# Queries and keys produced with features on partitions, RoPE by a lane shuffle

## The chip, the cores and the metric

The kernel runs on one core of one Trainium2 chip. The metric is the device time of one execution in microseconds (us). The core has a matrix engine (TensorE, PE in the profile, with its weight loads as PEld), a vector engine (VectorE, DVE), an activation engine (ScalarE, ACT), a general engine (GpSimd, POOL), and a queue engine (SyncE, SP) that here issues all DMAs. Each engine works through its own instructions in order; semaphores make one wait for another. Tiles lie in SBUF on 128 partitions; products land in PSUM banks of 128 x 512 f32.

## The reference

Everything is f32. x is 4 sequences of 512 tokens with 1024 features. Layernorms have no weights.

```python
x = x + layernorm(attention(layernorm(x)))
x = x + layernorm(ffn(layernorm(x)))

# attention: 32 query heads, 8 key/value heads of 32 features
qkv = x @ w_qkv.T + b_qkv                 # 1024 + 256 + 256 columns
q, k = apply_rope(q), apply_rope(k)       # turns pairs of features by a position's angle
scores = q @ k.T / sqrt(32), causal; out = softmax(scores) @ v
return out @ w_o.T + b_o

# ffn: a plain product plus 8 experts of rank 16, two chosen per token
result = x @ base_w.T + base_b
result += 2 * sum over e of w_full[e] * (x @ lora_A[e].T) @ lora_B[e].T
```

## The kernel before

**Tokens and staging.** The 2048 tokens are 16 tiles of 128, in the program `tokens`; four tiles are one sequence, and tile i of a sequence (i from 0 to 3) sees i + 1 blocks of keys. For each tile x is loaded (`xa`), normalised, and transposed on TensorE (`transposes`, line 562) to `T_xn`, which has features on partitions. The same is done for the input of the ffn (`T_h`). Tiles are worked on in pairs. The first tile of the last sequence is attended last.

**Products.** `project` (line 577) makes 128 x 512 of a product: for each of 8 (or 4) chunks of 128 features, one matmul with the tokens as the stationary operand (128 x 128, loaded as weights) and 512 weight columns moving (line 587). So the result has tokens on partitions. A pair of tiles goes through `seven` (line 626): the 2 x 2 block product of two tiles by two feature halves by two column halves is made with 7 block products in place of 8. It needs sums of input tiles (`s_q`, `s_o`, `s_f`, in `parts`) and mixed weight blocks, which `mix` makes at the start and writes to DRAM. Each of the 7 has 4 steps of one matmul. Bank results are added into the output tiles on VectorE (line 698); the bias and the difference of the bias's halves (`bias_step`) come in there. Bias tiles are copies of the row on all 128 partitions (`bqkv_sb`, 768 KB by one DMA). The first pair, and single tiles elsewhere, go through `whole`: 8 steps for each half of the columns. Weight pieces of 128 x 512 (`piece`) stream in through a ring of 14.

**Keys and values.** `keys_values` (line 888) makes k and v of a tile together: 8 steps with 512 columns (256 of k, 256 of v). VectorE adds the biases, v to its tile and k to `raw_k`; then come RoPE, two transposes on TensorE (line 929) and two copies to `kT`, which has features on partitions.

**Queries.** `queries` (line 953) makes q into `raw_q`, tokens on partitions, in two halves of 512 columns; then come RoPE, four transposes a half (line 980) and one copy on ScalarE to `qT` with the factor 1/sqrt(32) (line 987).

**RoPE.** The columns of a head are sorted, first components first. `rotate` (line 729) has VectorE multiply the swapped halves by sin (two instructions at line 740, into `turn`), then GpSimd multiply `raw` by cos in place (line 751), then VectorE add the two (line 756). `turn` has one buffer, `raw` six, shared by q and k.

**Attention.** A group is 4 heads, one from each quarter of the partitions, or 8 or 16 where a tile sees only two blocks of keys or one. `scores` (line 1347) makes the products of `qT` and `kT` in four PSUM banks that belong to all groups in turn (`sc`); VectorE adds the mask (line 1416) and takes maxima (line 1426), ScalarE takes exps with sums (line 1376), GpSimd scales (line 1390), TensorE transposes (line 1440), ScalarE or VectorE copies, and `values` multiplies by v (line 1463).

**What sets the order.** The order on every engine is fixed when the program is built. `Order` (line 90) plays the work through with an assumed duration for each instruction and appends each to its engine when its turn comes. On TensorE the scores come first, then the transposes (`turn_lanes`), then the values, then the dense products (`gl_lane`, `kv_lane`, `main_lane`), whichever is ready. `main_lane` is a fixed sequence: q of the first pairs, then for each pair its output product, q of the pair two later, and its ffn. On the other engines an instruction has an urgency (0 first). PSUM outside `sc` has 4 banks, taken and given by `banks`. SP issues the loads in the order of `all_loads` (line 1491) with the pieces between: x of the first tile, the k and v weights, then the qkv bias, then the RoPE table.

Of the kernel before, what the change touches and what calls it, by code (L numbers as in the profile page):

```python
# [260 lines left out]
def kernel(  # L261
# [34 lines left out]
    kvpool = ctx.enter_context(tc.tile_pool(name="kvpool", bufs=4))  # L296
# [12 lines left out]
    qT_slots, kT_slots, raw_slots, turn_slots = Slots(8), Slots(4), Slots(6), Slots(1)  # L309
# [55 lines left out]
    bqkv_sb = const.tile([P, QKV], F32, name="bqkv_sb")  # L365
# [13 lines left out]
    def loads(what):  # L379
# [16 lines left out]
    biases = {  # L396
        "q": bqkv_sb,
        "o": bo_sb,
        "f": bbase_sb,
    }  # L400
    bias_steps = {name: const.tile([P, 512], F32, name=f"bias_step_{name}") for name in plain}
# [39 lines left out]
    def bias_step(name):  # L441
        yield loaded["b", name]
        b = biases[name]
        yield combine(
            4, lambda: bias_steps[name], lambda: b[:, 512:D], lambda: b[:, :512], ALU.subtract
        )
        has_bias[name].finish(order.at)
# [150 lines left out]

    def with_pieces(used, steps):
        for piece, step in zip(used, steps):  # L600
            step.piece = piece
            start(piece.used(step.done))
        return steps

    def whole(name, tok_name, k, lhsT, ready, take, room, used=None, more=None):

        used = used or block(name, plain, 0, k) + block(name, plain, 1, k)
        needs = [[ready[c // 4], used[c].here] for c in range(ND)]
        needs[0] += room
        if more:  # L610
            needs.append(more[2])
        return with_pieces(
# [13 lines left out]
    def seven(name, pair_name, tiles, ready, out, room, ended, free, more=None):  # L626
# [17 lines left out]
        def parts(taken):  # L644
# [15 lines left out]
        bias = biases[name]  # L660
# [13 lines left out]
            (lambda: bias[:, :512], c11, None),  # L674
            (c11, c21, None),
            (c11, c11, None),
            (lambda: bias_steps[name], c22, None),
# [30 lines left out]
        for k, (lhs, wants, of, h, half) in enumerate(blocks):  # L708
# [11 lines left out]
            def w(c, used=used, extra=extra):  # L720
                return used[c].sb if c < H else extra[1]

            steps += with_pieces(
                used,
                project(lhsT, w, 512, f"{name}_{pair_name}_{k}", needs, partial(take, k)),
# [3 lines left out]
    def rotate(raw, n, i, name):  # L729

        nh, half = n // HD, HD // 2
        yield turn_slots.take()
        turn = ropes.tile([P, 512], F32, tag="turn", name=f"turn_{name}")
        raw3, turn3 = (a[:, :n].rearrange("p (h d) -> p h d", d=HD) for a in (raw, turn))
        for a, b in ((0, half), (half, 0)):
            sin = rope_sb[:, i, 1, a : a + half].unsqueeze(1).to_broadcast([P, nh, half])
            yield dve(
                0.1 + n * 0.00065,
                2,
                lambda: nc.vector.tensor_tensor(  # L740
                    out=turn3[:, :, a : a + half],
                    in0=raw3[:, :, b : b + half],
                    in1=sin,
                    op=ALU.mult,
                ),
            )
        cos = rope_sb[:, i, 0, :].unsqueeze(1).to_broadcast([P, nh, HD])
        yield pool(
            0.2 + n * 0.0021,
            1,  # L750
            lambda: nc.gpsimd.tensor_tensor(out=raw3, in0=raw3, in1=cos, op=ALU.mult),
        )
        yield dve(
            0.1 + n * 0.0012,
            2,
            lambda: nc.vector.tensor_add(raw[:, :n], raw[:, :n], turn[:, :n]),
        )
        turn_slots.give(order.at)

    def new_raw(name):  # L760
        return ropes.tile([P, 512], F32, tag="raw", bufs=6, name=f"raw_{name}")


    class Sequence:
        def __init__(self, b):
            self.kT = [None] * NKT
            self.kT_taken = [kT_slots.take() for _ in range(NKT)]
            self.has_k, self.v, self.has_v = {}, {}, {}
            self.b = b
            self.left = [NQ * GROUP] * NKT  # L770
            self.left_v = NQ * ND

        def k_tile(self, kt):
            if self.kT[kt] is None:
                self.kT[kt] = kvpool.tile([P, S], F32, tag="kT", name=f"kT_{self.b}_{kt}")
            return self.kT[kt]
# [111 lines left out]
    def keys_values(job):  # L888
# [3 lines left out]
        raw, has_raw, k_ready = [], Task(), Task()  # L892

        def take_raw():
            yield [job.ready[0]] + seq.kT_taken
            yield v_slots.take()
            yield raw_slots.take()
            has_raw.finish(order.at)

        start(take_raw())  # L900

        def take(acc, done):
            yield done
            job.read(order.at)

            def v_issue():
                seq.v[i] = kvpool.tile([P, KVD], F32, tag="v", bufs=6, name=f"v_{t}")
                nc.vector.tensor_add(
                    seq.v[i], acc[:, KVD : 2 * KVD], bqkv_sb[:, D + KVD : D + 2 * KVD]
                )  # L910

            yield dve(0.41, 0, v_issue)
            seq.has_v[i].finish(order.at)
            raw.append(new_raw(f"k_{t}"))
            yield dve(
                0.1 + KVD * 0.00115,
                0,
                lambda: nc.vector.tensor_add(
                    raw[0][:, :KVD], acc[:, :KVD], bqkv_sb[:, D : D + KVD]
                ),  # L920
            )
            banks.give(order.at)
            yield from rotate(raw[0], KVD, i, f"k_{t}")
            k_ready.finish(order.at)

        def turn_k():
            pt = ps.tile([P, 4, P], F32, tag="ps", name=f"pt_k_{t}")
            for kt in range(NKT):
                nc.tensor.transpose(pt[:, kt, :], raw[0][:, kt * P : (kt + 1) * P], ident)

            def end():
                yield step_k.done
                raw_slots.give(order.at)
                for kt in range(NKT):
                    yield copy(
                        P,
                        lambda: seq.k_tile(kt)[:, i * P : (i + 1) * P],
                        lambda: pt[:, kt, :],
                    )
                banks.give(order.at)  # L940
                seq.has_k[i].finish(order.at)

            start(end(), order.now)

        step_k = Step(0.23, turn_k, [k_ready], bank=True)
        needs = [[job.ready[c // 4], loaded["kv", c]] for c in range(ND)]
        needs[0] += [has_raw, loaded["b", "q"]]
        products = project(
            lambda c: job.xnT()[:, c, :], lambda c: wkv_sb[:, c, :], 2 * KVD, f"kv_{t}", needs, take
        )  # L950
        return [step_k], products

    def queries(pair, used=None):

        raw, q_ready, steps_q = {}, {}, {}

        def take_room():
            yield q_job[pair[0]].ready[0]
            for _ in range(NH * len(pair)):
                yield qT_slots.take()  # L960
                yield raw_slots.take()
            has_room.finish(order.at)

        has_room = Task()
        start(take_room())

        def out(k, h):
            if (k, h) not in raw:
                raw[k, h] = new_raw(f"q_{pair[k].t}_{h}")
            return raw[k, h]  # L970

        def ended(k, h):
            yield from rotate(raw[k, h], 512, pair[k].i, f"q_{pair[k].t}_{h}")
            q_ready[k, h].finish(order.at)

        def turn_q(k, h):
            tok = pair[k]
            pt = ps.tile([P, 4, P], F32, tag="ps", name=f"pt_q_{tok.t}_{h}")
            for c in range(4):
                nc.tensor.transpose(pt[:, c, :], raw[k, h][:, c * P : (c + 1) * P], ident)  # L980

            def end():
                yield steps_q[k, h].done
                raw_slots.give(order.at)
                tok.qT[h] = qpool.tile([P, 4, P], F32, tag="qT", name=f"qT_{tok.t}_{h}")
                yield act(
                    0.6, 0, lambda: nc.scalar.activation(tok.qT[h], pt, AF.Copy, scale=QSCALE)
                )
                banks.give(order.at)
                tok.has_q[h].finish(order.at)  # L990

            start(end(), order.now)

        for k, h in [(0, 0), (0, 1), (1, 0), (1, 1)][: NH * len(pair)]:
            q_ready[k, h] = Task()
            steps_q[k, h] = Step(0.44, partial(turn_q, k, h), [q_ready[k, h]], bank=True)
        names = [q_job[tok] for tok in pair]
        if len(pair) == 2:
            steps = seven(
# [9 lines left out]
            return [[steps_q[0, 0], steps_q[0, 1]], [steps_q[1, 1]], [steps_q[1, 0]]], steps  # L1009

        def take(h, acc, done):
# [3 lines left out]
            cols = slice(h * 512, (h + 1) * 512)  # L1015
            yield dve(0.69, 0, lambda: nc.vector.tensor_add(out(0, h), acc, bqkv_sb[:, cols]))
# [15 lines left out]
        return [[steps_q[0, 0], steps_q[0, 1]]], steps  # L1032
# [314 lines left out]
    def scores(g):  # L1347
# [4 lines left out]
        for c in range(g.n):  # L1352
            for r in range(QUADS):
# [4 lines left out]
                    rhs=seq.kT[g.kt][rows, :n],  # L1358
# [42 lines left out]
        def softmax():  # L1401
# [4 lines left out]
            seq.left[g.kt] -= g.n  # L1406
            if not seq.left[g.kt]:
# [83 lines left out]
    def all_loads():  # L1491
# [10 lines left out]
        bias_q = load(("b", "q"), 768, bqkv_sb, b_qkv.broadcast_to([P, QKV]))  # L1502
# [7 lines left out]
        def chain():  # L1510
# [3 lines left out]
            yield from loads([bias_q, rotary])  # L1514
# [64 lines left out]
    kv_lane, gl_lane, main_lane = [], [], []  # L1579
    for job in jobs:  # L1580
# [118 lines left out]
```

## Time and profile before

| | |
|---|---|
| median of three runs | 1208.66 us (1207.46 to 1209.03) |
| the profiled execution | 1208.46 us, its span 1206.7 us |
| granted TensorE clock | 0.987 of full |
| TensorE matmul records | 7248 |
| transposes of q (line 980) | 128 |
| transposes of k (line 929) | 32 |
| records of q's products | 456 |
| records of k and v's products | 256 |

The span runs from the first to the last instruction. A line of instructions reads: line of the program, engine, operation, output<-inputs, shape, count; then busy time in us and the mean of one in ns; then the idle time of the engine just before, and who ended it. In a list of instructions by tile or line the three numbers are shortest, median and longest in ns, then the first and last start. A wait reads: who waited <- for whom, us in total, times, longest. A line of the timeline is start, length, engine, line, operation, and how many like it follow one another. A line of a window is its bounds and length, then busy us (and instructions) of PE, PEld, DVE, ACT and POOL, the granted clock, DMA share and GB/s. One f32 matmul of the program is two records, a transpose is one. Matmuls are pipelined, so the time of one record is longer than the distance to the next.

### The profile page before, as it was taken

How to read it: one execution, taken by the hardware profiler on the slowest of the kernel's cores; microseconds unless marked ns; L12 is line 12 of the kernel's file. 1: busy time of each engine (PE TensorE's matmuls, PEld its weight loads, DVE VectorE, ACT ScalarE, POOL GpSimd, SP SyncE). 2: the span in 40 equal slices, each digit the busy share in tenths (PEclk: the TensorE clock that was granted, in tenths of full speed). 3: DMA queues.
4: the chain of work that ended last, by engine and by line, in shares of the span. 5: the costliest groups of instructions: out<-in, count | busy, mean ns of one | idle time of the engine just before them, and what ended most of it. 6: DMA issues, size and time to landing. Idle time of an engine off the chain costs nothing.

```text
span 1206.7 us, 21495 instructions
## 1 busy us (share of the span) xinstructions
PE 1154.6 (96%) x7248; PEld 630.9 (52%) x7248; DVE 908.3 (75%) x1932; ACT 452.9 (38%) x1399; POOL 614.8 (51%) x801
## 2 busy tenths in 40 slices
PE   6999899999899999999999999999999999979997
PEld 3545454645556555565555555555555555536453
DVE  4687887987768977898777777789777897676453
ACT  0344443443435344345433233344433443344000
POOL 1575866753555645454745445445545572554211
PEclk9999899999999999999999999999999999988999
DMA  9768768665174445754367355853347644733783
GB/s 347 257 223 297 253 216 279 222 217 182 54 225 142 149 149 175 235 162 157 128 207 237 124 177 172 271 171 129 105 124 254 208 137 153 269 115 99 254 309 122
DMA packets 118316, 232.52 MB, mean 193 GB/s; under 512 B 13504, under 2 KB 14528, under 8 KB 118208
## 3 DMA queue, kind: packets, MB, share of 16 engines
q1 hardware_dynamic: 118208, 231.16, 58.1%
q8 instruction: 58, 0.95, 0.3%
q14 instruction: 50, 0.41, 0.1%
HBM read 210.14 MB, written 20.97 MB: 192 GB/s over the span
## 4 chain that ended last, share of the span: by engine, by line
PE 77%; DVE 13%; ACT 3%; POOL 3%; issue 2%; DMA 2%; SPq 0%; POOLq 0%; ACTq 0%
PE acc_f L587 17%; PE acc_o L587 16%; PE acc_q L587 11%; PE pt_p L1440 10%; PE acc_kv L587 7%; PE sc L1355 6%; PE av L1463 5%; DVE nmax L1426 3%; ACT pr L1376 3%; DVE sc L1416 2%; PE acc_gl L587 2%; POOL pr L1390 2%; PE pt_xn L562 1%; PE pt_h L562 1%; DVE w L533 1%
## 5 line engine op out<-in xcount | busy, mean ns | idle before, releaser
L1390 POOL TENSOR_SCALAR pr<-pr,rtot 128x256 f32<-128x256 f32 (+3 forms) x512 | 310.7, 620 | 296.1 <-DVE rtot L1385 205.6
L1376 ACT ACTIVATE pr<-sc,nmax 128x256 f32<-128x256 f32 (+3 forms) x512 | 264.5, 532 | 209.4 <-DVE sc L1416 83.0
L1426 DVE TENSOR_REDUCE nmax<-sc 128x2 f32<-128x768 f32 (+3 forms) x176 | 198.2, 1126 | 48.1 <-ACT pr L1376 45.4
L1440 PE MATMUL pt_p<-ident,pr 128*128 128x128 f32 x1280 | 181.4, 279 | 16.6 <-POOL pr L1390 9.6
L1440 PEld LDWEIGHTS pt_p<-ident,pr 128*128 128x128 f32 x1280 | 146.7, 142 | 85.7 <-issue 52.2
L330 ACT COPY prT<-pt_p 128x512 f32<-128x512 f32 (+1 forms) x212 | 112.3, 545 | 190.4 <-PE pt_p L1440 189.3
L587 PE MATMUL acc_kv<-wkv_sb,T_xn 128*128 128x512 f32 x256 | 117.1, 596 | 0.2 <-DVE w L698 0.2
L331 DVE COPY prT<-pt_p 128x512 f32<-128x512 f32 (+1 forms) x140 | 89.9, 643 | 34.9 <-PE pt_p L1440 33.1
L587 PE MATMUL acc_q<-piece,T_xn 128*128 128x512 f32 x224 | 105.9, 599 | 3.3 <-DMA piece<-in_w_qkv_dram 3.0
L587 PE MATMUL acc_f<-piece,T_h 128*128 128x512 f32 x232 | 108.4, 597 | 0.2 <-ACT prT L330 0.2
L1376 ACT ACTIVATION_READ_ACCUMULATOR pr<-sc,nmax 128x1 f32 x512 | 106.7, 208 | 0.0
L587 PE MATMUL acc_f<-piece,s_f 128*128 128x512 f32 x224 | 106.5, 595 | 0.1
L587 PE MATMUL acc_o<-piece,aT 128*128 128x512 f32 x232 | 105.8, 600 | 0.0
L1416 DVE TENSOR_TENSOR sc<-sc,cmask 128x256 f32<-128x256 f32 (+2 forms) x176 | 96.5, 548 | 10.4 <-ACT pr L1376 4.8
L1355 PE MATMUL sc<-kT,qT 32*128 32x384 f32 (+3 forms) x1024 | 96.5, 476 | 7.8 <-ACT pr L1376 7.6
L587 PE MATMUL acc_q<-piece,s_q 128*128 128x512 f32 x224 | 103.5, 595 | 0.1
L587 PE MATMUL acc_o<-piece,s_o 128*128 128x512 f32 x224 | 102.2, 593 | 0.0
L522 POOL TENSOR_TENSOR rstd<-veps,neg_half 128x1 f32<-128x1 f32 x64 | 35.5, 558 | 115.3 <-DVE veps L518 115.3
L1385 DVE RECIPROCAL rtot<-total 128x1 f32<-128x1 f32 (+2 forms) x352 | 53.9, 158 | 51.2 <-ACT pr L1376 49.1
L1463 PEld LDWEIGHTS av<-prT,v 128*32 128x32 f32 x2560 | 65.3, 109 | 51.2 <-issue 39.5
L1463 PE MATMUL av<-prT,v 128*32 128x128 f32 x2560 | 90.5, 276 | 0.0
L338 POOL TENSOR_TENSOR y<-y,w 128x512 f32<-128x512 f32 x60 | 79.4, 1334 | 17.1 <-DVE w L533 17.0
(146 smaller groups left out, 1390.0 us busy)
## 6 DMA issues: line engine op xcount, KB each, us to landing
piece<-in_w_o_dram SPq DMA_DIRECT2D x116, 256.0 KB, 3.5
piece<-in_w_base_dram SPq DMA_DIRECT2D x116, 256.0 KB, 3.6
piece<-mixed_q SPq DMA_DIRECT2D x112, 256.0 KB, 3.6
piece<-mixed_o SPq DMA_DIRECT2D x112, 256.0 KB, 3.8
piece<-mixed_f SPq DMA_DIRECT2D x112, 256.0 KB, 3.2
piece<-in_w_qkv_dram SPq DMA_DIRECT2D x100, 256.0 KB, 3.6
xa<-in_x_dram SPq DMA_DIRECT2D x32, 256.0 KB, 3.7
y<-in_x_dram SPq DMA_DIRECT2D x16, 512.0 KB, 4.8
```

The lines of the kernel that those rows point to most:

```text
L330: act=(0.15 + n * 0.00085, lambda: nc.scalar.copy(out(), in_())),
L331: dve=(0.15 + n * 0.00105, lambda: nc.vector.tensor_copy(out(), in_())),
L338: engine.tensor_tensor(out=out(), in0=in0(), in1=in1(), op=op)
L587: nc.tensor.matmul(acc[0][:, :n], lhsT=lhsT(c), rhs=w(c), start=(c == 0), stop=last)
L1355: nc.tensor.matmul(sc[:, r, c * n : (c + 1) * n], lhsT=tok.qT[g.kt][rows, (g.at + c) % GROUP, :], rhs=seq.kT[g.kt][rows, :n], start=True, ...
L1376: lambda: nc.scalar.activation(pr[:, c * n : (c + 1) * n], sc4[:, r, c, :], AF.Exp, bias=nmax[:, r, c : c + 1], accum_out=total[:, r, c : ...
L1385: yield dve(0.17, 1, lambda: nc.vector.reciprocal(rtot[:, r, : g.n], total[:, r, : g.n]))
L1390: lambda: nc.gpsimd.tensor_scalar(pr[:, c * n : (c + 1) * n], pr[:, c * n : (c + 1) * n], rtot[:, r, c : c + 1], 1.0, ALU.mult, ALU.mult,),
L1416: lambda: nc.vector.tensor_tensor(out=diag, in0=diag, in1=cmask.unsqueeze(1).unsqueeze(1).to_broadcast([P, q, g.n, P]), op=ALU.add,),
L1426: lambda: nc.vector.tensor_reduce(nmax[:, some, : g.n], sc4[:, some], AX.X, ALU.max, negate=True),
L1440: nc.tensor.transpose(pt[:, j, :], g.pr[r][:, j * P : (j + 1) * P], ident)
L1463: nc.tensor.matmul(av[r * HD : (r + 1) * HD, c, :], lhsT=g.seq.v[j][:, head * HD : (head + 1) * HD], rhs=g.prT[r][:, c * (i + 1) + j, :], ...
```

## The change

Products of q and k have the weights as the stationary operand and x moving. A step of q that was one matmul with 512 moving columns is four, each with 128 weight columns as stationary operand and the 128 tokens moving, into four quarters of the bank. Results have features on partitions, so the transposes and their copies are gone. q is accumulated in `qT` itself. k has 4 steps (two halves of 128 features, each in two steps of 4 matmuls), v has 4 steps with tokens stationary as before, 256 columns moving; they share one bank.

The biases of q and k are one number per partition: `bqk_sb`, 128 x 10, loaded from the row by a DMA of single elements; v's bias is a copy on all partitions. For q, VectorE adds it spread along the tokens; for k, ScalarE adds it while it copies from PSUM.

RoPE's swap of halves is a shuffle of 32 lanes on VectorE. The tables of sin and cos are turned once at the start: GpSimd repeats the 32 columns of each four times, TensorE transposes it (8 transposes in all), ScalarE copies it with the factor 32^(-1/4), so that q and k together carry 1/sqrt(32). GpSimd's cos multiply and VectorE's sin multiply both follow the shuffle. `turn` has two buffers. `kT` is one tile for a sequence. SP issues the table ahead of the biases.

```diff
+    def project_turned(x, w, name, needs, take):
...
+        def issue(c):
...
+            for f in range(4):
+                nc.tensor.matmul(
+                    acc[0][:, f, :],
+                    lhsT=w(c)[:, f * P : (f + 1) * P],
+                    rhs=x(c),
...
         ends = (
-            (lambda: bias[:, :512], c11, None),
+            (bias(biases[name]), c11, None),
...
-    def rotate(raw, n, i, name):
-
-        nh, half = n // HD, HD // 2
+    SWAP = [(d + HD // 2) % HD for d in range(HD)]
+
+    def rotate(raw, out, i, name):
...
+        def multiply(t, by, engine):
+            engine.tensor_tensor(out=t, in0=t, in1=by, op=ALU.mult)
+
+        yield dve(0.1 + n * 0.135, 2, lambda: nc.vector.stream_shuffle(turn, raw, SWAP))
+
+        def by_cos():
+            yield pool(0.2 + n * 0.27, 1, partial(multiply, raw, cos, nc.gpsimd))
+
+        has_cos = start(by_cos(), order.at)
+        yield [loaded["sin"]]
+        yield dve(0.1 + n * 0.145, 2, partial(multiply, turn, sin, nc.vector))
+        yield has_cos
         yield dve(
-            0.1 + n * 0.0012,
+            0.1 + n * 0.155,
             2,
-            lambda: nc.vector.tensor_add(raw[:, :n], raw[:, :n], turn[:, :n]),
+            lambda: nc.vector.tensor_tensor(out=out(), in0=raw, in1=turn, op=ALU.add),
         )
         turn_slots.give(order.at)
...
+    def rope_tables():
...
+                    nc.gpsimd.tensor_copy(
+                        wide[0].rearrange("p i (r d) -> p i r d", d=HD)[:, :NQ],
+                        rope_sb[:, :, at, :].unsqueeze(2).to_broadcast([P, NQ, QUADS, HD]),
+                    )
...
+                for i in range(NQ):
+                    nc.tensor.transpose(pt[:, i, :], wide[0][:, i, :], ident)
...
+                        lambda: nc.scalar.activation(
+                            to, pt[:, :NQ], AF.Copy, scale=math.sqrt(QSCALE)
+                        ),
...
     def keys_values(job):
...
+            if n < 4:
+                kt = n // 2
+                for c in range(4 * (n % 2), 4 * (n % 2) + 4):
+                    nc.tensor.matmul(
+                        acc[0][:, kt * P : (kt + 1) * P],
+                        lhsT=wkv_sb[:, c, kt * P : (kt + 1) * P],
+                        rhs=job.xnT()[:, c, :],
...
+            else:
+                for c in range(2 * (n - 4), 2 * (n - 4) + 2):
+                    nc.tensor.matmul(
+                        acc[0][:, half : half + KVD],
+                        lhsT=job.xnT()[:, c, :],
+                        rhs=wkv_sb[:, c, half : half + KVD],
...
+            for kt in range(NKT):
+                yield act(
+                    0.3,
+                    1,
+                    lambda: nc.scalar.activation(
+                        raw[:, kt, :],
+                        acc[:, kt * P : (kt + 1) * P],
+                        AF.Identity,
+                        bias=bqk_sb[:, ND + kt : ND + kt + 1],
+                    ),
+                )
+            start(keys(raw), order.at)
...
-        def turn_k():
-            pt = ps.tile([P, 4, P], F32, tag="ps", name=f"pt_k_{t}")
-            for kt in range(NKT):
-                nc.tensor.transpose(pt[:, kt, :], raw[0][:, kt * P : (kt + 1) * P], ident)
...
     def queries(pair, used=None):
...
         def ended(k, h):
-            yield from rotate(raw[k, h], 512, pair[k].i, f"q_{pair[k].t}_{h}")
-            q_ready[k, h].finish(order.at)
-
-        def turn_q(k, h):
             tok = pair[k]
-            pt = ps.tile([P, 4, P], F32, tag="ps", name=f"pt_q_{tok.t}_{h}")
-            for c in range(4):
-                nc.tensor.transpose(pt[:, c, :], raw[k, h][:, c * P : (c + 1) * P], ident)
...
+            yield [loaded["cos"], loaded["sin"]]
+            yield from rotate(out(k, h), lambda: out(k, h), tok.i, f"q_{tok.t}_{h}")
+            tok.has_q[h].finish(order.at)
...
-        bias_q = load(("b", "q"), 768, bqkv_sb, b_qkv.broadcast_to([P, QKV]))
+        biases_qkv = [
+            load(
+                ("b", "q"),
+                128,
+                bqk_sb,
+                b_qkv[:, : D + NKT * P].rearrange("o (f p) -> p (o f)", p=P),
+            ),
+            load("bv", 128, bv_sb, b_qkv[:, D + KVD :].broadcast_to([P, KVD])),
+        ]
...
-            yield from loads([bias_q, rotary])
+            yield from loads([rotary] + biases_qkv)
```

## The prediction

> **What bounds it now.** I read the page first: the busy line, then the chain that ended last.
>
> ```profile
> PE 1154.6 (96%) x7248; PEld 630.9 (52%) x7248; DVE 908.3 (75%) x1932; ACT 452.9 (38%) x1399; POOL 614.8 (51%) x801
> ...
> PE 77%; DVE 13%; ACT 3%; POOL 3%; issue 2%; DMA 2%; SPq 0%; POOLq 0%; ACTq 0%
> ```
>
> TensorE (PE) is full and holds 77% of the chain, so its bill comes first. Busy times overlap (a matmul drains while the next starts), so I price a record by the pitch of a run, from the timeline of TensorE in two windows (start, length, instructions):
>
> ```profile
> 602.35 3.60 PE L587 MATMUL acc_kv<-wkv_sb,T_xn 128*128 128x512 f32 x8
> 605.78 3.60 PE L587 MATMUL acc_f<-piece,s_f 128*128 128x512 f32 x8
> ...
> 611.67 1.91 PE L1440 MATMUL pt_p<-ident,pr 128*128 128x128 f32 x16
> 613.42 3.60 PE L587 MATMUL acc_f<-piece,T_h 128*128 128x512 f32 x8
> ```
>
> ```profile
> 240.63 2.12 PE L587 MATMUL acc_gl<-wgl_sb,T_h 128*128 128x136 f32 x16
> 242.59 0.59 PE L587 MATMUL acc_f<-piece,T_h 128*128 128x512 f32 x1
> ```
>
> A record with 512 moving columns costs (605.78 - 602.35)/8 = 0.429 us, a 128-column transpose (613.42 - 611.67)/16 = 0.109. The 136-column run takes 0.1225 each; single starts in the trace show 0.22 for its first record, which waits for its weights, and 0.116 for the rest. One f32 product is two such records, each with its own weight load. The slope between 136 and 512 columns is 0.313/376 = 0.83 ns a column, so 128 columns should cost 0.109.
>
> Two waits decide who else sets the pace: those of TensorE's matmuls, and those of its weight loads (PEld) between 712 and 1085 us.
>
> ```profile
> PE pt_q L980 <- DVE raw_q L756: 2.2, 2, 1.1
> ...
> PE pt_k L929 <- DVE veps L518: 1.0, 1, 1.0
> ```
>
> ```profile
> PEld sc L1355 <- ACT pr L1376: 18.3, 16, 7.0
> ```
>
> In the late stretch a score product (sc) waits 16 times for the exps of the group before it to free its bank: there attention's own chain (mask, maximum, exps) paces, and dense products fill TensorE between. Earlier it is the other way about. The timeline near 670 us has
>
> ```profile
> 670.25 0.60 PE L980 MATMUL pt_q<-ident,raw_q 128*128 128x128 f32 x4
> ...
> 672.38 0.93 PE L1355 MATMUL sc<-kT,qT 32*128 32x384 f32 x8
> ```
>
> the first scores of tokens 10 and 11, only 2.1 us after their q was transposed, and 32 us after the scores before them (640.02): attention waited for q, that is for TensorE. So I call the kernel TensorE-paced up to about 712 and attention-paced from there to about 1085, where dense work runs out (TensorE idles 6.75 us before 1079).
>
> **The change, part by part.**
>
> *Transposes of q and k go (L980, L929).* 128 + 32 records x 0.109 = 17.4 us of TensorE. Their waits (2.2 and 1.6 us, by their groups) go or pass to the next instruction; I count half, 1.9.
>
> *q's products are cut in four.* 228 steps (224 + 224 + 8 records, two a step) went at 2 x 0.429 = 0.858. Now a step is 8 records of 128 columns with 8 weight loads. The lower end is 0.109 a record; the upper is the 136-column pitch, 0.116. Weight loads in this trace never start closer than 0.108 to 0.110, so I take 0.110: 0.880 a step, +0.022 x 228 = +5.0 us (0.116 makes +16.0). Here a rule speaks against the change: the Trainium skill, "TensorE: Matmul & The Clock Gate", § Back-to-back issue gap, gives about 81 ns for an N=128 matmul in a stream of load-and-multiply pairs, where the isolated gap is 56: 25 ns of surcharge. On 0.109 that makes 0.134, a step of 1.07, and +49 us for q alone. The gl run is just such a stream (own weights each time) and fits the column slope without a surcharge, so I follow the row.
>
> *k and v.* A token had 16 records x 0.429 = 6.86 us. Now k has 32 x 0.110 = 3.52 and v 16 records of 256 columns at 0.116 + 120 x 0.00083 = 0.216, 3.45: 6.97, +0.11 x 16 = +1.7 us (+4.8 at 0.116). The tables add 8 transposes, 0.9.
>
> TensorE's sum: -17.4 + 5.0 + 1.7 + 0.9 = **-9.8 us**. By stretch: before 712 lie 24 of 32 q rotations, 13 of 16 k and 172 of 228 steps: -13.3 + 3.8 + 1.4 + 0.9 = -7.2. After it -2.6; attention paces there, so I count half, -1.3.
>
> *RoPE on VectorE (DVE) and GpSimd (POOL).* The rows of the lines now used, for line 740, line 756, and the groups view for line 751:
>
> ```profile
> L740 DVE TENSOR_TENSOR turn_q<-raw_q,rope_sb x64: 369/418/1483, 29.3 to 1003.7; 128x256 f32<-128x256 f32 x64
> L756 DVE TENSOR_TENSOR raw_q<-raw_q,turn_q x32: 666/681/1244, 31.5 to 1005.8; 128x512 f32<-128x512 f32 x32
> ```
>
> ```profile
> L751 POOL TENSOR_TENSOR raw_q<-raw_q,rope_sb 128x512 f32<-128x512 f32 x32 | 42.7, 1335 | 16.9 <-DVE turn_q L740 16.2 <-DVE w L1155 0.4 <-DVE gmax L1130 0.4
> ```
>
> A q rotation takes 2 x 0.418 + 0.681 = 1.52 us of DVE at medians. After: a shuffle (not in the trace; nearest is the 128x512 copy, 0.69, which I take; the Trainium skill's "VectorE: DVE Perf Modes", § The perf-mode tier table, has about 2.4 us for 2048 elements, an estimate of 0.6; the upper end is two copies, 1.4, as if a second pass were needed), a multiply at 0.68 and the add, 0.68: 2.05, +0.53. k: two multiplies 0.56, bias add 0.41, add 0.51 and some 0.25 of copies of kT go to 0.42 + 0.42 + 0.51: -0.38. There is a second cost. The cos multiply on POOL (1.27 undisturbed) overwrites raw, so it starts when the shuffle ends, just when DVE's sin multiply is ready; before, POOL's multiply came behind DVE's two. The Trainium skill, "SBUF — State Buffer", § Who interferes with whom, says that a DVE instruction with two SBUF inputs and a GpSimd one that reads SBUF exclude each other for a whole instruction, the later one waiting. The rows agree on the size (the maxima, 1483 and 1244, lie 1.07 and 0.56 above their medians), but their median is undisturbed and L740's mean, 545, is 0.13 above it. By the rule each q rotation loses up to 1.27 on DVE, 41 us in all; by the row 0.13. If DVE goes first, POOL waits and nobody else does; I take 0.4. So +0.93 a q rotation and about -0.2 a k one. Up to 712 this lies beside TensorE's backlog (DVE 78% busy there by the windows) and costs nothing; with that cover gone it is 24 x 0.93 = 22. Between 712 and 1085 there are 8 q and 3 k rotations: +7 us on a DVE that is 80% busy:
>
> ```profile
> 712.00:848.00 136.00, 133.57 (x902) 73.15 (x902) 109.10 (x238) 57.44 (x151) 66.51 (x78) 1.00 0.53 173
> ```
>
> What queues behind a blocked multiply there is the mask, the maximum, the PSUM copies, and behind these the exps that free the score bank. A quarter on the path: **+1.7**. ScalarE (ACT) sheds 32 qT copies (19.1) and 18 kT copies (4.3) and gains 32 biased copies of 128 columns (nearest the 128-column exp, 0.39: 12.4); at 38% busy, nothing.
>
> *The start.* SP now issues rope before the biases, and q's bias is 1280 runs of 4 bytes in place of 768 KB.
>
> ```profile
> rope_sb<-in_rope_dram SPq DMA_DIRECT2D x1, 128.0 KB, 6.5
> ```
>
> Issued at about 6.4 where the bias went, rope lands near 12.9; two widening copies on POOL (as its 512-element multiply, 1.27 each) end at 14.2 and 15.5. TensorE works from 12.0 in order; if the table transposes stand early in its queue it waits, and the k, v and q products behind them. Between 0 and 3.5 us; I take **+1.0**. The 4-byte runs: all packets average 11217/118208 = 0.095 us of an engine (58.1% of 16 engines over the span), so 80 per engine cost at most 7.6 against 2.3 for the 768 KB. Pieces issued from 7.0 are used from 21.3, which hides that; DVE's bias step stands in front of the second token's statistics (16.42) and could hold them up to 5 us. Taken at 0.
>
> **Sum**: -7.2 - 1.3 - 1.9 + 1.7 + 1.0 = -7.7 us. The profiled execution took 1208.46 (span 1206.7 and 1.8 around it), 0.2 under the median of the three runs: 1208.46 - 7.7 = **1200.8**. A measurement of this kernel tells about 0.2%, 2.4 us, from no change.
>
> **Rivals.**
> - *More comes through (8%)*: TensorE paces to the end, and q ready without transpose and copy shortens each handover like that at 670. All of -9.8 and of the 3.8 us of waits: 1195.
> - *Absorbed (17%)*: attention's chain paces everywhere and removed work turns into idle, as the 6.75 us at 1079 suggests; the tight handover at 670 speaks against it. 1208, 1205 to 1211.
> - *Weights don't hide (10%)*: at 0.116 a record the bill is -17.4 + 16.0 + 4.8 + 0.9 = +4.3, about 1214 with the start. The spacing of 0.109 in transposes speaks against it, though those load in 0.14 and f32 weights in 0.19.
> - *Slower: the sin multiply blocked by its own cos multiply (15%)*. Place: VectorE's queue between a q rotation and the next mask or maximum. Price: 1.27 x 32 = 41 us of DVE; if a third reaches the score bank, +14 on the -9.4 that the sum has without its +1.7: 1213. It decides against the change once the mean loss on the path passes 9.4/32 = 0.29 us a rotation.
>
> **How the numbers follow.** The forecast has 50%, its own range 1194 to 1205. Faster: 50 + 8 + 3 of the absorbed = 61%; same: 10 of the absorbed; slower: 4 + 10 + 15 = 29%. Leaving one in ten out on each side: 1193 to 1216.
>
> **What would show it.** Right: records of acc_q 0.109 to 0.112 apart, no pt_q or pt_k, TensorE's busy time down by about 10 us, the sin multiply's mean under 1.1 us. Wrong: a pitch of 0.116 or more; a sin multiply near 1.9 us with the sc waits on ACT up; more TensorE idle in place of the transposes; or a table reload on ACT, with which I reckon nowhere (one load of 1.28 us now). An order of instructions that comes out otherwise for its own reasons could move the time by some us either way.

## The result: slower by 1.4%

The changed kernel takes 1226.27 us (1223.09 to 1228.64) where the kernel before takes 1208.85 in the same session: a ratio of 1.0143, interval 1.0115 to 1.0170, so +17.4 us where -7.7 was forecast. The profiled execution has a span of 1223.3 us. The page's busy line and the chain that ended last, after:

```profile
PE 1153.2 (94%) x8976; PEld 804.3 (66%) x8976; DVE 920.8 (75%) x1948; ACT 439.6 (36%) x1375; POOL 630.6 (52%) x813
...
PE 75%; DVE 13%; ACT 3%; POOL 3%; DMA 2%; issue 2%; SPq 0%; POOLq 0%; ACTq 0%; DVEq 0%
```

TensorE is busy 1.4 us less than before. What is not busy grew from 1206.7 - 1154.6 = 52.1 to 1223.3 - 1153.2 = 70.1 us: the span's +16.6 is -1.4 of work and +18.0 of idle. So there are two questions: why the work fell by so little, and where the idle comes from.

The pitch of the new records, from the timeline of TensorE after:

```profile
599.79 2.96 PE L1004 MATMUL acc_kv<-T_xn,wkv_sb 128*128 128x128 f32 x25
602.59 1.68 PE L1013 MATMUL acc_kv<-wkv_sb,T_xn 128*128 128x256 f32 x7
```

(602.59 - 599.79)/25 = 0.112 us, against 0.110 in the sum. A q step costs 0.896, +0.038 and not +0.022, so the bill is -17.4 + 8.7 + 2.9 + 0.9 = -4.9 us and not -9.8.

The rest of the difference to -1.4 went with the granted clock, whose mean is 0.983 after and 0.987 before. TensorE after, from 89 us, and a window there (the clock is the third number from the end):

```profile
89.05 1.09 PE L565 MATMUL pt_xn<-ident,xa 128*128 128x128 f32 x4 [4.56 <-DVE xa L536]
89.92 1.06 PE L1531 MATMUL pt_p<-ident,pr 128*128 128x128 f32 x4
```

```profile
89.00:92.00 3.00, 2.95 (x14) 2.98 (x15) 1.40 (x4) 1.50 (x7) 2.53 (x4) 0.50 0.65 242
```

At a clock of 0.50 four transposes take 0.87 us, 0.22 each and not 0.109. Before has three such stretches between its start and its end, after has six; each begins within a wait of TensorE or at most 1.1 us behind one. Their lengths and TensorE's busy time in them add up, before and then after, to:

```profile
sum 27.31, PE 18.95 PEld 11.22 DVE 18.64 ACT 9.66 POOL 22.54; mean PE 6.32 PEld 3.74 DVE 6.21 ACT 3.22 POOL 7.51
sum 37.54, PE 25.86 PEld 21.07 DVE 23.98 ACT 17.87 POOL 23.19; mean PE 4.31 PEld 3.51 DVE 4.00 ACT 2.98 POOL 3.86
```

If all of it takes twice as long there, as those transposes do, half of 25.86 - 18.95 is an estimate of what that adds: 3.5 us, and -4.9 + 3.5 is the -1.4. The clock doesn't explain the result, though: the four runs have 0.978 to 0.988, and the one at 0.988 still took 1223.09.

The waits of TensorE, after (who waited <- for whom, us in total, times, longest):

```profile
PE pt_xn L565 <- DVE xa L536: 11.4, 2, 6.8
PE sc L1446 <- ACT pr L1467: 10.1, 2, 9.8
...
PE pt_p L1531 <- DVE qT L746: 8.6, 5, 2.5
PE pt_h L565 <- DVE tied L1236: 5.7, 1, 5.7
PE pt_p L1531 <- ACT prT L330: 4.2, 6, 1.0
```

Before, these stood at 8.1, 7.6, 1.6 (on raw_q), 1.8 (on w) and 0.8. Three of them lead to the causes. The first is pt_p waiting for VectorE's line 746, which empties q's PSUM banks. VectorE, GpSimd and TensorE around 243 us after:

```profile
241.76 0.68 DVE L338 TENSOR_TENSOR mix_f<-mix_f 128x512 f32<-128x512 f32 x1
...
242.91 1.80 DVE L793 TENSOR_TENSOR turn_q<-turn_q,sin_sb 128x512 f32<-128x512 f32 x1
244.63 0.42 DVE L1507 TENSOR_TENSOR sc<-sc,cmask 128x256 f32<-128x256 f32 x1
...
246.23 0.68 DVE L746 TENSOR_TENSOR qT<-acc_q,qT 128x512 f32<-128x512 f32 x1
```

```profile
242.89 1.28 POOL L793 TENSOR_TENSOR qT<-qT,cos_sb 128x512 f32<-128x512 f32 x1
```

```profile
243.97 0.60 PE L1531 MATMUL pt_p<-ident,pr 128*128 128x128 f32 x4
247.06 2.34 PE L1531 MATMUL pt_p<-ident,pr 128*128 128x128 f32 x10 [2.49 <-DVE qT L746]
```

GpSimd's cos multiply starts 0.02 us ahead of VectorE's sin multiply, which then takes 1.80 in place of 0.69. The mask, the maximum and the add that empties q's bank stand behind it, and TensorE, next in want of a bank, idles 2.49 us. Over all 32, the multiplies of line 793 (shortest, median, longest in ns):

```profile
L793 DVE TENSOR_TENSOR turn_q<-turn_q,sin_sb x32: 665/692/1796, 31.0 to 999.7; 128x512 f32<-128x512 f32 x32
L793 POOL TENSOR_TENSOR qT<-qT,cos_sb x32: 1264/1274/1775, 31.1 to 999.6; 128x512 f32<-128x512 f32 x32
```

The sin multiply's mean is 994 ns: 0.30 us above its median, near the 0.4 assumed; the add's mean of 918 lies 0.24 above the 681 of before's. Not all of it is the cos multiply's: without that, below, the sin multiply's mean is still 787.

The second is the end of attention. TensorE's score and h records there, before and then after:

```profile
1079.48 2.09 PE L1355 MATMUL sc<-kT,qT 32*128 32x512 f32 x8 [6.75 <-ACT pr L1376]
1087.44 1.11 PE L562 MATMUL pt_h<-ident,w 128*128 128x128 f32 x4 [1.80 <-DVE w L533]
```

```profile
1091.59 2.09 PE L1446 MATMUL sc<-kT,qT 32*128 32x512 f32 x8 [9.80 <-ACT pr L1467]
...
1115.19 1.09 PE L565 MATMUL pt_h<-ident,w 128*128 128x128 f32 x4 [5.66 <-DVE tied L1236]
```

Dense work has run out in both, and TensorE waits for the last exps and for the input of the ffn: 8.6 us before, 15.5 after, +6.9.

The third is the wait of 4.56 us that ends at 89.05, for a normalised x (`xa`). Between 40 and 130 us the waits for `xa` are 1.1 us before and 4.6 after.

### The profile page after: what moved, and what is told of

Its sections match the earlier page's. It is cut to its first block, busy times and chain, and to the rows that moved or that the text cites. A ratio compares the mean times of both kernels' runs of the same rounds, so it can differ in the third digit from the quotient of the medians.

```text
span 1223.3 us, 25031 instructions
## 1 busy us (share of the span) xinstructions
PE 1153.2 (94%) x8976; PEld 804.3 (66%) x8976; DVE 920.8 (75%) x1948; ACT 439.6 (36%) x1375; POOL 630.6 (52%) x813
## 4 chain that ended last, share of the span: by engine, by line
PE 75%; DVE 13%; ACT 3%; POOL 3%; DMA 2%; issue 2%; SPq 0%; POOLq 0%; ACTq 0%; DVEq 0%
PE acc_f L590 17%; PE acc_o L590 15%; PE acc_q L613 11%; PE pt_p L1531 10%; PE sc L1446 6%; PE av L1554 5%; DVE nmax L1517 4%; PE acc_kv L1004 4%; PE acc_kv L1013 3%; ACT pr L1467 3%; POOL pr L1481 2%; DVE sc L1507 2%; PE acc_gl L590 2%; PE pt_h L565 1%; PE pt_xn L565 1%
## 5 line engine op out<-in xcount | busy, mean ns | idle before, releaser
L1481 POOL TENSOR_SCALAR pr<-pr,rtot 128x256 f32<-128x256 f32 (+3 forms) x512 | 314.6, 628 | 308.5 <-DVE rtot L1476 210.1
L1531 PE MATMUL pt_p<-ident,pr 128*128 128x128 f32 x1280 | 184.7, 281 | 26.8 <-POOL pr L1481 9.6
L331 DVE COPY prT<-pt_p 128x512 f32<-128x512 f32 (+1 forms) x145 | 92.5, 640 | 35.5 <-PE pt_p L1531 32.9
L613 PE MATMUL acc_q<-T_xn,piece 128*128 128x128 f32 x896 | 111.1, 279 | 4.6 <-DMA piece<-in_w_qkv_dram 2.8
L613 PEld LDWEIGHTS acc_q<-T_xn,piece 128*128 128x128 f32 x896 | 106.5, 194 | 9.2 <-issue 6.0
L613 PE MATMUL acc_q<-s_q,piece 128*128 128x128 f32 x896 | 108.0, 275 | 0.0
L1446 PE MATMUL sc<-kT,qT 32*128 32x384 f32 (+3 forms) x1024 | 96.4, 475 | 10.1 <-ACT pr L1467 10.1
L613 PEld LDWEIGHTS acc_q<-s_q,piece 128*128 128x128 f32 x896 | 104.1, 192 | 0.6 <-issue 0.4
L1554 PEld LDWEIGHTS av<-prT,v 128*32 128x32 f32 x2560 | 65.7, 109 | 52.1 <-issue 38.2
```

What stands on the lines that cost most here:

```text
L331: dve=(0.15 + n * 0.00105, lambda: nc.vector.tensor_copy(out(), in_())),
L613: nc.tensor.matmul(acc[0][:, f, :], lhsT=w(c)[:, f * P : (f + 1) * P], rhs=x(c),  start=(c == 0 and f == 0), stop=last, skip_group_check=True,
L1446: nc.tensor.matmul(sc[:, r, c * n : (c + 1) * n], lhsT=tok.qT[g.kt][rows, (g.at + c) % GROUP, :], rhs=seq.kT[rows, g.kt, :n], start=True, ...
L1481: lambda: nc.gpsimd.tensor_scalar(pr[:, c * n : (c + 1) * n], pr[:, c * n : (c + 1) * n], rtot[:, r, c : c + 1], 1.0, ALU.mult, ALU.mult,),
L1531: nc.tensor.transpose(pt[:, j, :], g.pr[r][:, j * P : (j + 1) * P], ident)
L1554: nc.tensor.matmul(av[r * HD : (r + 1) * HD, c, :], lhsT=g.seq.v[j][:, head * HD : (head + 1) * HD], rhs=g.prT[r][:, c * (i + 1) + j, :], ...
```

## The experiments

Theory E: VectorE's sin multiply and GpSimd's cos multiply exclude each other, and what queues behind them on VectorE stops TensorE. Theory P: the products' cut records cost it. Theory O: the order that the program works out for itself came out worse, whatever the instructions.

**The products alone.** In the kernel before, in `project`:

```diff
-            nc.tensor.matmul(
-                acc[0][:, :n], lhsT=lhsT(c), rhs=w(c), start=(c == 0), stop=last
-            )
+            cuts = [(0, n)]
+            if name.startswith("q_"):
+                cuts = [(f * P, P) for f in range(4)]
+            if name.startswith("kv_"):
+                cuts = [(0, P), (P, P), (2 * P, 2 * P)]
+            for at, m in cuts:
+                nc.tensor.matmul(
+                    acc[0][:, at : at + m],
+                    lhsT=lhsT(c),
+                    rhs=w(c)[:, at : at + m],
...
```

> The kernel before, its order of work unchanged, with each q product of 512 moving columns cut into four of 128 (and k's 256 into two), tokens still stationary: the changed kernel's matmul records and weight loads without anything else of it. At the pitch of 0.112 us that the changed kernel shows, TensorE gets 228 x 0.038 + 16 x 0.18 = 11.5 us more work. Theory 'the products cost it' (TensorE paces): about 1220, +11. Theory 'the lane of attention paces and rotations on VectorE cost it': +0 to +5, 1209 to 1214.

Measured 1214.72, ratio 1.0043 (1.0028 to 1.0058): +5.0 us for 11.5 us of added TensorE work. The page shows the work arriving, 1154.6 to 1165.0:

```profile
PE 1165.0 (96%) x9128; PEld 813.3 (67%) x9128; DVE 907.9 (75%) x1932; ACT 453.6 (37%) x1399; POOL 613.6 (51%) x801
```

The added work counted at 0.43 of its length (0.29 to 0.61 by the interval). Theory P alone falls: with the transposes gone the changed kernel has less of that work than before.

**Without the cos multiply.** In the changed kernel's `by_cos`:

```diff
-            yield pool(0.2 + n * 0.27, 1, partial(multiply, raw, cos, nc.gpsimd))
+            yield pool(0.2 + n * 0.27, 1, lambda: None)
```

> The changed kernel, order unchanged, with GpSimd's cos multiply left out (results are then not rotated rightly), so nothing stands beside VectorE's sin multiply. Theory 'the sin multiply is blocked by its own cos multiply': the sin multiply falls from 0.99 to under 0.8 us and the time by most of the loss, to about 1212 to 1217. Theory 'order or products': within 3 us of 1226.

Measured 1213.56, 1.0041 of before (1.0028 to 1.0054): -12.7. The sin multiply's mean falls from 994 to 787 ns. E is borne out, but GpSimd also has 56 us less to do.

**Without the rotation.** Shuffle and sin multiply are emptied in the same way, and the add takes `in1=raw`.

> The changed kernel, order unchanged, with shuffle, sin and cos multiply left out; the add stays (adding the tile to itself). It takes 63 us off VectorE and 56 off GpSimd. If VectorE's and GpSimd's rotation is what makes the changed kernel slower, it falls to 1205 or below; if TensorE's bill or the planned order does it, it stays above 1215.

Measured 1207.20, 0.9982 of before (0.9972 to 0.9992): another -6.4 with VectorE busy 50 us less. It missed the 1205, and the waits of 9.8 and 5.7 us at the end of attention and of 4.6 us for `xa` are still there: they don't come from the rotation. Even without its rotation the changed kernel is only level with the kernel before, which has its own.

**GpSimd as busy, but not reading.**

```diff
-            yield pool(0.2 + n * 0.27, 1, partial(multiply, raw, cos, nc.gpsimd))
+            def fill():
+                for _ in range(3):
+                    nc.gpsimd.memset(raw, 0.5)
+
+            yield pool(0.2 + n * 0.27, 1, fill)
```

> The changed kernel, order unchanged, with GpSimd's cos multiply replaced by three fills of the same tile (the cos product is left out): GpSimd is busy about as long at the same place and later work waits for it alike, but it reads nothing from SBUF. If the two multiplies exclude each other by their reads, this runs like the version without the multiply, near 1213 to 1216, with a sin multiply under 0.8 us. If GpSimd's time itself is what costs, it stays near 1226.

Measured 1216.95, 1.0044 (1.0025 to 1.0063): -9.3, one us above what was expected, with GpSimd busy 631.2 us (630.6 in the changed kernel). The three fills of a q rotation take 1.60 us, longer than the multiply's mean of 1.35. The sin multiply, same line, is nearly free of stalls (mean 734):

```profile
L793 DVE TENSOR_TENSOR turn_q<-turn_q,sin_sb x32: 671/683/1345, 32.3 to 992.9; 128x512 f32<-128x512 f32 x32
```

So it is the reading, not the time on GpSimd. Between the two profiles the span falls by 7.2 us. The wait of pt_p on line 746 falls from 8.6 to 4.1 us, and of the stretches at half clock 30.7 us are left of 37.5; the one behind the wait of 2.49 us is gone. The same edit in another order of the work:

> The changed kernel in the order of FILL 0.28 (1214), with the cos multiply replaced by three fills that read nothing (the cos product is left out), order unchanged. In the order of 0.30 this took 9 us off. If the exclusion costs that in any order: 1203 to 1208. If the saving belonged to that one order: 1211 to 1215.

Measured 1202.69 against 1214.03: -11.3, with the sin multiply's mean at 695 in place of 897. The control is the same edit in the kernel before (line 751), in two orders:

> A control: the kernel before, order unchanged, with its cos multiply on GpSimd replaced by three fills of the same tile (the cos product is left out). If the exclusion is what the change brought in, the kernel before has little of it to lose: 1206 to 1209. If before pays for it just as much, it falls by 9 to 11 as the changed kernel does, to about 1199, and the exclusion doesn't tell the two kernels apart.

> The same control in before's order with FILL at 0.28 (1225). Exclusion brought in by the change: 1221 to 1225. Exclusion in both alike: about 1215.

Measured 1211.72 (+3, its fills being longer than the multiply) and 1219.21 (-6 from 1225.41); the first lies above what was expected, the second between the two expectations. The mean is -2 in the kernel before and -10 in the changed one. Before's sin multiplies aren't freed by it (means 545 to 536 ns, and 512 to 535 in the second order), so they don't explain the -6, whose cause stays open. With it, it isn't shown that the whole of the changed kernel's gain is the change's own.

**The order.** `FILL` is a delay that the program assumes between a matmul's end and its use. Changing it by 0.01 leaves the work and TensorE's 8976 records as they are and gives another order; a few copies and sums go to another engine (at 0.28 VectorE has 1944 instructions in place of 1948, GpSimd 798 in place of 813).

```diff
-FILL = 0.3
+FILL = 0.29
```

> The changed kernel with one assumed delay of the plan at 0.29 us in place of 0.30 (FILL): the same instructions in another order; the plan's clock ends 2 us earlier. It measures what the order alone moves. If orders differ by luck by 1%, it may lie anywhere from 1214 to 1234; if the loss is in the instructions, 1222 to 1228.

> The kernel before with FILL at 0.29 in place of 0.30: the same instructions in another order; the plan's clock ends 3 us later. If 1209 was a lucky order, 1215 to 1222; if not, 1207 to 1213.

> The kernel before in the order that the plan makes with FILL at 0.28; the plan's clock ends 2 us later than before's. So far before's two orders measured 1209 and 1220. Theory 'before's order was one of the lucky ones of its kind': 1213 to 1222. Theory 'orders of before lie near 1209, 0.29 is an outlier': 1206 to 1212.

> The kernel before with FILL at 0.31; the plan's clock ends 1 us later. The same two theories: 1213 to 1222 or 1206 to 1212.

> The changed kernel with FILL at 0.28; the plan's clock ends 6 us earlier than with 0.30. If the instructions make the loss (two multiplies that exclude each other) it shows in every order: 1218 to 1228, above the before kernel's mean. If the order makes it, this one may fall to 1212.

> The changed kernel with FILL at 0.31; the plan's clock ends as with 0.30. Instructions: 1222 to 1232. Order: anywhere from 1212 to 1234.

In the last column cos is planned behind sin:

```diff
-        has_cos = start(by_cos(), order.at)
-        yield [loaded["sin"]]
+        yield [loaded["cos"], loaded["sin"]]
         yield dve(0.1 + n * 0.145, 2, partial(multiply, turn, sin, nc.vector))
-        yield has_cos
+        yield from by_cos()
```

> The changed kernel with the cos multiply planned behind the sin multiply, not beside it; the order of work comes out anew. The plan's own clock ends TensorE's work 10 us earlier than with the changed kernel's order. Theory 'blocked by its own cos multiply': sin multiply near 0.75 us and 1212 or less. Theory 'luck of the order': about 1216, by the plan alone. Theory 'products': 1224 to 1228.

> The changed kernel with cos behind sin and FILL at 0.28; the plan's clock ends 7 us earlier than with 0.30 (1165.8 against 1172.6; that order measured 1210). If the plan's clock counts, 1203 to 1207 and faster than before; if luck of the order dominates, 1200 to 1222. Against the cos-beside-sin kernel at 0.28 (1214), theory 'the two multiplies exclude each other' wants it lower.

> The same at FILL 0.29 (plan 1170.7). Exclusion theory: well under the 1231 of cos beside sin at 0.29, about 1208 to 1218. Order alone: no tendency, 1208 to 1232.

> The same at FILL 0.31 (plan 1177.9). Exclusion theory: under the 1226 of cos beside sin at 0.31, about 1210 to 1220. Order alone: no tendency.

Medians in us:

| FILL | before | changed | cos behind sin |
|---|---|---|---|
| 0.28 | 1225.41 | 1214.03 | 1201.17 |
| 0.29 | 1220.05 | 1231.24 | 1209.14 |
| 0.30 | 1208.85 | 1226.27 | 1210.21 |
| 0.31 | 1206.77 | 1225.99 | 1223.19 |
| mean | 1215.3 | 1224.4 | 1210.9 |

One hundredth in a delay moves a kernel by up to 17 us, as much as the whole result. Of the expectations, before at 0.28 lies above both of its ranges, cos behind sin at 0.31 above that of the exclusion, and the changed kernel at 0.28 between its two. Over the four settings the changed kernel is 9 us above before, with differences from -11 to +19, so the sign of the change itself isn't settled by them. Cos behind sin is under cos beside sin in all four, by 2.8 to 22.1, mean 13.5. That is not E alone: its sin multiplies, expected near 750 ns, still average 918 (0.30) and 889 ns (0.28), and its order differs. At 0.28 they average 897 with cos beside sin, much the same, and yet the kernel takes 12.9 us longer.

One part of the difference is the same in every order. Between 40 and 130 us TensorE waits 4.6 to 6.1 us for `xa` in all four orders with cos beside sin (4.6 without the cos multiply too), at most 1.1 in before's four, and not at all with cos behind sin. So this wait comes with a plan that puts the two side by side, and not with the exclusion.

The bad end of attention belongs to the order: the kernel before has it at 0.28. Its waits of TensorE between 1050 and 1130 us:

```profile
PE sc L1355 <- ACT pr L1376: 10.1, 2, 9.8
PE pt_h L562 <- DVE tied L1145: 5.2, 1, 5.2
```

The changed kernel lacks it at 0.28, its fastest.

**True durations for the plan.**

> The changed kernel with cos behind sin, and with the plan told the durations that were measured (a q step 0.896 us, shuffle 0.73, sin multiply 0.91, cos 1.40, add 0.81). The plan's clock now ends TensorE's work at 1193 against 1172.6 with cos behind sin and the old durations (which measured 1210). If true durations make a better order: 1200 to 1207. If the plan's clock counts, with the lag of some 15 us of the kernel before: 1213 to 1220.

```diff
-            steps.append(Step(0.872, partial(issue, c), needs[c], bank=(c == 0)))
+            steps.append(Step(0.896, partial(issue, c), needs[c], bank=(c == 0)))
...
-        yield dve(0.1 + n * 0.135, 2, lambda: nc.vector.stream_shuffle(turn, raw, SWAP))
+        yield dve(0.14 + n * 0.1475, 2, lambda: nc.vector.stream_shuffle(turn, raw, SWAP))
...
```

Measured 1224.85, 1.0112 (1.0091 to 1.0133): above both expectations, and no better for knowing the durations. The plan's own clock ends TensorE's work at 1193 here and at 1182.7 for the changed kernel, 10 us apart, where the chip shows 1 (1226).

**A version that beats both.** Cos behind sin at FILL 0.28: 1201.17, ratio 0.9932 (0.9917 to 0.9946). TensorE is busy 1145.9 us in a span of 1199.4:

```profile
PE 1145.9 (96%) x8976; PEld 799.2 (67%) x8976; DVE 909.6 (76%) x1932; ACT 443.8 (37%) x1390; POOL 630.9 (53%) x814
```

It is the best of four orders, so part of it is luck; the best of before's four is 1206.77.

## Why the prediction was wrong

*TensorE's sum, -9.8, of which 8.5 counted.* Right in kind (no transposes of q and k are left, no surcharge of 25 ns), too large: the pitch was 0.112 (the spacing of weight loads that 0.110 rested on holds for those of 128x128; the 128x32 ones of `av` start 0.02 us apart), the bill -4.9, and with the stretches at half clock the busy time fell by 1.4. And its worth was overrated. I called TensorE the pace up to 712 us and counted each microsecond there in full; added work showed 0.43 of its length. The removed work met idle instead, and on the plan already: on the clock of the plan that the program makes as it is built, and that knows no exclusion, TensorE's work shrinks by 12.1 us from before to after while its idle grows by 11.7, from 48.5 to 60.3. On the plan, then, the rival "absorbed" held for this part.

*RoPE, +1.7: this is the step that failed first.* The exclusion and the loss per sin multiply were foreseen (0.30 for 0.4). The reading of before's row was not right: its 0.13 is for one of two half multiplies, so a rotation lost 0.25. Nor was the cover: "Up to 712 this lies beside TensorE's backlog ... and costs nothing". A dense step also needs VectorE, to empty its bank, in VectorE's order; a blocked multiply ahead of it leaves TensorE without a bank, backlog or not. Of the 8.6 us that pt_p waits for q's banks, 5.5 lie before 712. With the order held, taking the cos multiply's reads away gains 9.3 and 11.3 us where the term had 1.7. The slower rival had the block and 1213, but another path, by the score bank, and that one didn't lengthen: the waits of the scores' weight loads for the exps, without the longest, which is the end of attention, are 31.8 - 7.0 = 24.8 us before and 29.8 - 10.1 = 19.7 after.

*The shuffle, 0.69 taken.* 0.73, with 0.01 for loading its pattern. *The start, +1.0.* Nothing: the table transposes run at 15.12 between products, and the 4-byte bias lands within 4.9 us. *No table reload*: one load, as before.

*What no step had.* The end of attention, +6.9 us of idle, comes from the order, and so do the 3.5 us more for `xa`; I named an order that comes out otherwise and gave it "some us". The measured spread of one kernel's orders, 17 to 19 us, is wider than the forecast's own range of 11. Exclusion (9.3), end (6.9) and `xa` (3.5), less the bill's 4.9, make 14.8 of the 17.4. That they simply add isn't shown, and the stretches at half clock belong in part to each. One run points that way: in the order of 0.28, which lacks the bad end, and with fills in place of the cos multiply, the changed kernel measures 1202.7, near the forecast of 1200.8. The remaining differences between orders are not traced.

## What to carry to other kernels

Where a program works out its own order, time it in several orders before judging a change: a difference of 1% between two single orders says little about the instructions. Work that one engine does "beside" a full TensorE isn't covered if the same engine empties TensorE's banks in order: price a stall there by what stands behind it in the queue. Two multiplies released by the same instruction on VectorE and GpSimd met here in the q rotations (the sin multiply's mean was 994 ns, its median 692), and putting one behind the other in the plan is worth trying.

## What the runs showed of the hardware

f32 records of 128 columns with their own weights run 0.112 us apart, 2 to 3 ns more than transposes of the same size at 0.109 to 0.110. A VectorE multiply with two SBUF inputs took 0.69 us alone and up to 1.80 beside a GpSimd multiply that reads SBUF; beside fills, which only write and took longer in all, its mean was 0.73. The Trainium skill's "SBUF — State Buffer", § Who interferes with whom, says that a VectorE instruction with two SBUF inputs contends with a GpSimd instruction that reads SBUF and not with one that only writes it, and here it holds. After a wait of TensorE of 4.56 us the granted clock stood at 0.50 and a transpose took 0.22 us in place of 0.109. A 32-lane shuffle of 128x512 f32 took 0.73 us, a biased copy of 128x128 from PSUM on ScalarE 0.38, and a widening copy of 128x512 on GpSimd 0.61 where its multiply takes 1.27.
